# A recurrence on one core: block products of x in 384 columns on pairs of column tiles

## Chip, core and metric

One core of a Trainium2 chip. The time is that of one execution on the device, in microseconds. The engines are PE (matrix products; its weight loads are listed as PEld), DVE (vector), ACT (scalar functions and copies), POOL and SP (here it issues DMAs).

## The reference

A gated recurrence over T = 512 steps, for a batch of 8 and 512 units; its states are added to x:

```python
def step(h, x_t):
    fused = sigmoid(concatenate([x_t, h], -1) @ w_W + w_b)
    hidden_state, output_state = split(fused, 2, axis=-1)      # r and z below
    memory_state = x_t @ wx_W + wx_b + hidden_state * (h @ wh_W + wh_b)
    h_new = output_state * h + (1.0 - output_state) * tanh(memory_state)
    return h_new, h_new
return x + scan(step, cond_1024, x)        # x: (8, 512, 512) float32
```

So each step needs h @ [wh, r, z], 512 x 1536 weights, which can only start when the step before has ended, and x_t @ [wx, r, z], which depends on no state and can be done ahead.

## The kernel before

**Column tiles.** The batch is 8, so a stationary operand has few columns. PE is used as four column tiles of 32: the output's partitions 32j to 32j + 31 are tile j, which holds the units of quarter j. Each of the four tiles streams its own 128-row piece of weights as the moving operand, and they run side by side. All is float32.

**A step.** `ORDER` lists the recurrent products of step i: bank A (192 columns: half a of wh, z and r), B (128: r and wh of half b) and C (64: z of half b), each for four k (quarters of h) and four tiles j. k = 0, 1 are in `hT[0]` (hTA), k = 2, 3 in `hT[1]` (hTB). They accumulate in PSUM onto x's part, which ACT has copied there (`spread`). Then half a: DVE turns r (`tr`, L385), h (`md1`, L401) and z (`tz`); ACT takes sigmoids (md0, hd0); DVE scans give `m`, ACT takes tanh, and DVE scans give the new state (`update`, L369). Half b follows in the same way. ACT copies the new state (`hTB<-hTB`), and after that the step's extra work is issued: copies of ACT, turns and sums of DVE, sums of POOL. It thus runs while PE does the next step's A products. The order on each engine is written out by hand.

**x products.** A group `g` is four steps, 32 columns of x (4 steps x batch 8), and a block `o` is two groups, eight steps; u is the step's number in its block. The first groups are done plainly (`prefill`: 16 matmuls of 384 columns a group). From block 2 on, the 512 x 384 weights of a tile and the two groups of a block are taken as 2 x 2 blocks, and seven products with sums of weights (`tw`) and of x (`sx`, POOL, `x_sum`) replace eight. Here the weights' columns are halved within each tile: every product is 2 (k) x 4 (tiles) matmuls of 192 columns. They add into four regions, AL, BE, GA, DE, each 128 partitions by 192 columns of two PSUM banks (`xps`). `x_side` makes one long sequence of all these matmuls, and each step takes seven of it after its C products (`take(later, 7)`). Seven on four tiles are uneven, so `turn` moves the tile with which a step begins on by seven.

**Sums.** Part of the additions between regions is done in PSUM by ACT copies from region to region, part by DVE into `even` and `odd` in SBUF, from which (or from `xps`) `spread` fills the A, B and C banks and `turn_x` the x part of the memory state. The PSUM banks are A, B and C twice, for even and odd groups, and two for `xps`.

Of the kernel before, what the change touches and what calls it, by code (L numbers as in the profile page):

```python
# [40 lines left out]
def tile_cond_rnn_residual(  # L41
# [48 lines left out]
    psum = ctx.enter_context(tc.tile_pool(name="psum", bufs=1, space=PSUM))  # L90
# [43 lines left out]
    wx = const.tile([P, NQ, NQ, 384], F32, name="wx")  # L134
# [41 lines left out]
        nc.gpsimd.memset(t_[:, :, :, 1], -1.0)  # L176
    idle = const.tile([P, IDLE], F32, name="idle")

    tw = [const.tile([P, 2, NQ, HALF], F32, name=f"tw{n}") for n in range(4)]
    sx = [[const.tile([P, 2, GS * B], F32, name=f"sx{n}{q}") for q in range(2)] for n in range(4)]  # L180
    step_bias = const.tile([P, HALF], F32, name="stepbias")
    even = const.tile([P, 256], F32, name="even")
    odd = [const.tile([P, 256], F32, name=f"odd{q}") for q in range(2)]
    both = const.tile([P, HALF], F32, name="both")

    def state(hf, i, slot=2):

# [1 line left out]
        return hT[hf][i % NH][:, B * s : B * s + B, :, slot]  # L189

    ctx.enter_context(tc.manual_schedule())
    banks = [
        {n: psum.tile([P, w], F32, name=f"{n}{q}") for n, w in BANKS.items()}
        for q in range(2)
    ]
    xps = [psum.tile([P, 512], F32, name=f"xp{q}") for q in range(2)]

    def mm(out_, lhsT, rhs, start=False):
        nc.tensor.matmul(  # L199
            out_, lhsT, rhs, start=start, stop=False, skip_group_check=True  # L200
        )


    for t_ in list(banks[0].values()) + list(banks[1].values()):
        mm(t_, none, none[:, :1].broadcast_to([P, t_.shape[1]]), start=True)
    def warm():

# [4 lines left out]
    mm(xps[0], ones.rearrange("p j m -> p (j m)"), rows4, start=True)  # L212
    bias = const.tile([P, 512], F32, name="bias")
    nc.vector.tensor_copy(bias, xps[0])  # L214
# [5 lines left out]
    turn = [0]  # L220

# [11 lines left out]
    def seed(g):  # L233

        nc.scalar.copy(xps[g % 2], bias)  # L235

    def prefill(g):

        c, t0 = divmod(g * GS, TC)
        for k in range(NQ):  # L240
            for j in range(NQ):
                mm(
                    xps[g % 2][32 * j : 32 * j + 32, 64:448],
                    x_of(c, k, t0, GS),
                    wx[:, k, j, :],
                )
            yield

    def late(g):

        if g == 0:
            return xps[0][:, 256:512]
        return even if g % 2 == 0 else odd[g // 2 % 2]

    def part(g, c0, c1):

        return late(g)[:, c0 - 256 : c1 - 256] if c0 >= 256 else xps[g % 2][:, c0:c1]

    def spread(g, names):

        for n in names:
            nc.scalar.copy(banks[g % 2][n], part(g, XP[n].start, XP[n].stop))

    def turn_x(g, e):

        c0 = XP["X"].start + 32 * e
        nc.vector.transpose(md1[e // 2][g % 2][:, :, e % 2, 1], part(g, c0, c0 + 32))

    def reg(r):
        return xps[r[0]][:, r[1]]  # L270
# [8 lines left out]
    def weight_sum(n, k=slice(0, 2), j=None):  # L279
# [7 lines left out]
        at = (slice(0, P), k, slice(0, NQ) if j is None else slice(2 * j, 2 * j + 2))  # L287
        nc.vector.tensor_tensor(tw[n][at], a[at], b[at], ALU.subtract)
# [12 lines left out]
    def products(o):  # L301

        t_ = [q[o % 2] for q in sx]
        for to, lhs, rhs in (
            (AL, x_half(o, 0, 0), wx_of(0, 0)),
            (DE, t_[0], tw[0]),
            (BE, t_[1], tw[1]),
            (AL, x_half(o, 0, 1), wx_of(1, 0)),
            (GA, t_[2], tw[2]),
            (BE, t_[3], wx_of(1, 1)),  # L310
            (GA, x_half(o, 1, 1), tw[3]),
        ):
# [11 lines left out]
    def x_side():  # L324
        for o in range(2, NG // 2):
            yield from products(o)

    seed(1)
    take(prefill(0))
    warm()  # L330
    later = x_side()
    first = {g: prefill(g) for g in (1, 2, 3)}
    weight_sum(0)
    weight_sum(2)
    spread(0, "BCA")
    for e in range(NQ):
        turn_x(0, e)

    pool_done = {}
    for i in range(T):  # L340
# [8 lines left out]
        for n in (ORDER if i else FIRST).split():  # L349
            if n == "x":  # L350
                take(first[1], 1)
                continue
            bank, k = n[0], int(n[1])
            hs = hT[k // 2][i % NH][:, :, k % 2, 2]
            for j in range(NQ):
                j = (j + turn[0]) % NQ
                to = ps[bank] if i or bank != "A" else xps[0][:, XP["A"]]
                mm(to[32 * j : 32 * j + 32, :], hs, wh(bank, k, j))
        if i < 5:
            take(first[(i + 3) // 2], 2)  # L360
        else:
            take(later, 7)
            turn[0] += 7

        rows = slice(B * s, B * s + B)

# [99 lines left out]
        o, u = divmod(i, 2 * GS)  # L466
        nxt, two = o + 1 < NG // 2, o + 2 < NG // 2
        if i == 0:
            nc.scalar.copy(odd[0], xps[1][:, 256:512])
            spread(1, "A")  # L470
            turn_x(1, 0)
        ahead = 2 * o + (1 if u < 3 else 2 if u < 7 else 3)
        if ahead < NG:
            turn_x(ahead, (u + 1) % GS)
        if u == 0:
            spread(2 * o + 1, "B")
            if o and nxt:
                nc.scalar.copy(reg(GA), reg(BE))
        elif u == 1:
            spread(2 * o + 1, "C")  # L480
        elif u == 2 and o == 0:
            seed(3)
            nc.scalar.copy(even, xps[0][:, 256:512])
        elif u == 2 and nxt:
            last = odd[(o + 1) % 2][:, :HALF]
            nc.vector.tensor_tensor(last, reg(GA), both, ALU.add)
        elif u == 3 and nxt:
            if o:
                nc.vector.tensor_tensor(even[:, :HALF], reg(BE), both, ALU.add)
            spread(2 * o + 2, "A")  # L490
        elif u == 4 and nxt:
            if o == 0:
                nc.scalar.copy(odd[1], xps[1][:, 256:512])
            spread(2 * o + 2, "B")
            if two:
                nc.scalar.copy(reg(AL), bias[:, AL[1]])
                x_sum(o + 2, 0)
        elif u == 5 and nxt:
            spread(2 * o + 2, "C")
            if two:  # L500
                nc.scalar.copy(reg(DE), step_bias)
                x_sum(o + 2, 1)
        elif u == 6 and two:
            nc.scalar.copy(reg(BE), reg(AL))
            x_sum(o + 2, 2)
        elif u == 7 and nxt:
            spread(2 * o + 3, "A")
            if two:
                nc.scalar.copy(both, reg(DE))
# [3 lines left out]
        if i == 4:  # L513
            nc.gpsimd.tensor_tensor(step_bias, bias[:, BE[1]], bias[:, AL[1]], ALU.subtract)
        for n in range(IDLE - 1):
            nc.vector.memset(idle[:, n : n + 1], 0.0)
        def add(hf, engine):
# [97 lines left out]
```

## Time and profile before

| | |
|---|---|
| median of 3 runs | 1671.9 us (1671.46 to 1673.14) |
| profiled execution | 1671.53 us, its span 1669.5 us |
| granted TensorE clock | 0.999 in the mean |
| steps with block products | 496, from 38.37 to 1633.94 us |

Times in rows are microseconds from the span's start unless marked ns. A row of the timeline gives start, length, engine, line, operation, output<-inputs by the program's names, shape and count of merged instructions, and in brackets the idle time before and what ended it. A row of groups gives the count, then busy time, mean ns of one, and idle time before with what ended it. In the waits view a row gives who waited for whom, total, count and longest.

### The profile page before, as it was taken

The page shows a single profiled execution, that of the slowest core. Times are in us where ns is not written, and L with a number is a line of the kernel's source. Part 1 is how long each engine was busy: PE and PEld are TensorE (multiplying, and loading weights), DVE is VectorE, ACT ScalarE, POOL GpSimd, SP SyncE. Part 2 cuts the span into 40 slices and gives each one's busy share as a digit, 9 for nine tenths or more (in the row PEclk, how much of TensorE's full clock was granted, in tenths as well). Part 3 has the DMA queues.
Part 4 walks back from the last instruction along what each step waited for, and adds up shares of the span by engine and source line. Part 5 has one row for each costly group of instructions (what it writes and reads, how often), then busy time and mean ns, then how long its engine had stood idle before and what let it go on. Part 6 is the DMA issues. An engine that isn't in the chain of part 4 may idle for free.

```text
span 1669.5 us, 130236 instructions
## 1 busy us (share of the span) xinstructions
PE 1658.5 (99%) x56238; PEld 1639.1 (98%) x56238; DVE 1090.2 (65%) x9387; ACT 1029.7 (62%) x5822; POOL 301.7 (18%) x1281
## 2 busy tenths in 40 slices
PE   8999999999999999999999999999999999999998
PEld 5999999999999999999999999999999999999997
DVE  6666666666666666666666666666666666666666
ACT  3666666666666666666666666666666666666665
POOL 1111111111111111111111111111111111111111
PEclk9999999999999999999999999999999999999999
DMA  4000000000000000000000000000000000000000
GB/s 181 11 15 17 15 15 15 17 15 15 14 17 15 15 14 18 14 14 15 18 15 15 14 16 16 15 14 18 15 14 14 18 15 15 15 16 12 10 10 10
DMA packets 37304, 31.43 MB, mean 19 GB/s; under 512 B 4084, under 2 KB 35060, under 8 KB 36600
## 3 DMA queue, kind: packets, MB, share of 16 engines
q1 hardware_dynamic: 36576, 22.95, 4.4%
q8 instruction: 440, 7.21, 1.8%
q14 instruction: 136, 1.11, 0.2%
q10 hardware_dynamic: 152, 0.16, 0.0%
HBM read 14.70 MB, written 8.39 MB: 14 GB/s over the span
## 4 chain that ended last, share of the span: by engine, by line
PE 98%; DVE 1%; DMA 0%; issue 0%; ACT 0%
PE A L199 44%; PE B L199 23%; PE xp L199 20%; PE C L199 12%; DMA rows<-in_bias_dram 0%; DVE tr L385 0%; DVE m L369 0%; DVE tz L385 0%; DVE md1B L401 0%; DVE hTA L369 0%; DVE md1A L401 0%; DVE bias L214 0%; ACT hTB L227 0%; ACT xp L235 0%; DVE rows L131 0%
## 5 line engine op out<-in xcount | busy, mean ns | idle before, releaser
L199 PE MATMUL A<-wa,hTA 128*32 128x192 f32 x8176 | 639.0, 329 | 2.3 <-DVE hTA L369 2.3
L199 PE MATMUL B<-wb,hTA 128*32 128x128 f32 x8192 | 575.2, 273 | 0.0
L199 PE MATMUL A<-wa,hTB 128*32 128x192 f32 x8176 | 508.0, 326 | 0.4 <-DVE hTB L369 0.4
L199 PEld LDWEIGHTS B<-wb,hTA 128*32 128x32 f32 x8192 | 472.9, 122 | 1.1
L385 DVE STREAM_TRANSPOSE tr<-A 128x64 f32<-128x64 f32 x511 | 127.7, 250 | 462.5 <-PE A L199 462.5
L199 PE MATMUL B<-wb,hTB 128*32 128x128 f32 x8192 | 399.5, 273 | 0.0
L199 PEld LDWEIGHTS A<-wa,hTA 128*32 128x32 f32 x8176 | 386.8, 123 | 6.6 <-DVE hTA L369 4.0
L199 PEld LDWEIGHTS A<-wa,hTB 128*32 128x32 f32 x8176 | 373.6, 122 | 2.5 <-DVE hTB L369 0.8
L227 ACT ACTIVATE md0A<-tr 128x16 f32<-128x16 f32 x512 | 112.2, 219 | 419.9 <-DVE tr L385 419.9
L518 POOL TENSOR_TENSOR ot<-xin,hTB 128x16 f32<-128x16 f32 x503 | 125.9, 250 | 1323.4 <-DVE hTB L369 1312.9
L199 PEld LDWEIGHTS B<-wb,hTB 128*32 128x32 f32 x8192 | 322.3, 122 | 0.0
L199 PE MATMUL C<-wb,hTA 128*32 128x64 f32 x8192 | 290.2, 219 | 0.0
L199 PE MATMUL C<-wb,hTB 128*32 128x64 f32 x8192 | 289.7, 220 | 0.1
L199 PEld LDWEIGHTS C<-wb,hTA 128*32 128x32 f32 x8192 | 267.7, 122 | 0.0
L199 PE MATMUL xp<-tw,sx 128*32 128x192 f32 x2976 | 237.5, 326 | 0.0
L199 PEld LDWEIGHTS C<-wb,hTB 128*32 128x32 f32 x8192 | 229.8, 123 | 0.3 <-issue 0.3
L369 DVE TENSOR_TENSOR_SCAN hTB<-hd0B,hTB 128x24 f32<-128x24 f32 x1024 | 157.8, 196 | 100.9 <-ACT hTB L227 99.8
L369 DVE TENSOR_TENSOR_SCAN hTA<-hd0A,hTA 128x24 f32<-128x24 f32 x1024 | 191.9, 187 | 0.0
L199 PE MATMUL xp<-wx,xin 128*32 128x192 f32 (+1 forms) x2048 | 180.9, 331 | 0.0
L227 ACT ACTIVATE hd0B<-tz 128x16 f32<-128x16 f32 x512 | 115.2, 225 | 93.4 <-DVE tz L385 93.4
L227 ACT ACTIVATE hTB<-hTB 128x16 f32<-128x16 f32 x512 | 120.5, 235 | 79.8 <-DVE hTB L369 73.7
L227 ACT ACTIVATE hTB<-m 128x8 f32<-128x8 f32 x1024 | 160.6, 206 | 0.0
(92 smaller groups left out, 2491.0 us busy)
## 6 DMA issues: line engine op xcount, KB each, us to landing
out_dram<-ot SPq DMA_DIRECT2D x128, 64.0 KB, 2.0
xin<-in_x_dram SPq DMA_DIRECT2D x112, 64.0 KB, 2.5
wx<-in_wx_dram SPq DMA_DIRECT2D x4, 768.0 KB, 7.0
wa<-in_wa_dram SPq DMA_DIRECT2D x4, 384.0 KB, 8.9
wb<-in_wb_dram SPq DMA_DIRECT2D x1, 1152.0 KB
xin<-in_x_dram SPq DMA_DIRECT2D x3, 256.0 KB, 8.5
wb<-in_wb_dram SPq DMA_DIRECT2D x1, 384.0 KB, 10.9
head<-in_xh_dram ACTq DMA_DIRECT2D x1, 144.0 KB, 5.0
```

What stands on the lines that cost most here:

```text
L199: nc.tensor.matmul(out_, lhsT, rhs, start=start, stop=False, skip_group_check=True)
L227: inst = nc.scalar.activation(out_, in_, func, **kw).ins
L369: return nc.vector.tensor_tensor_scan(*[t_[:, :, c_].rearrange("p n c s -> p (n c s)") for t_ in (out_, d0, d1)], 0.0, ALU.mult, ALU.add,).ins
L385: inst = nc.vector.transpose(t_.rearrange("p c n -> p (c n)"), raw[n][hf]).ins
L518: return engine.tensor_tensor(ot[:, t, 2 * hf : 2 * hf + 2, :].rearrange("p c n -> p n c"), x_of(c, slice(2 * hf, 2 * hf + 2), t, 1).rearr ...
```

## The change

The weights' columns are no longer halved within each tile, but by tiles: the column halves of the 2 x 2 scheme are tiles 0, 1 and 2, 3 (`wx_of`). A product is then 2 (k) x 2 (tiles) matmuls of 384 columns, on the lower or the upper 64 partitions (`LO`, `HI`), and two products run side by side, one on each pair of tiles. `SLOTS` lists the seven pairs, 384 columns each. AL and GA are the lower, BE and DE the upper partitions of the two `xps` banks. One half of P5 (`E`) goes to a bank of its own, `eps`. To make room, the two C banks become one (`cs`), z of even and odd groups beside each other. `x_step` gives each step a share of columns of the sequence of slots: `SHARE`, 384 columns in steps u = 0, 1, 2 and 7 and 288 in u = 3 to 6; a piece that crosses the end of a slot is cut in two. `turn` goes.

The additions become eight ACT copies and three DVE sums of 64 x 384 per block, placed anew over the steps; `even` and `odd` hold all 512 columns, one buffer each, and every `spread` and `turn_x` reads them from SBUF (group 0 still from `xps`). `turn_x` turns 64 columns at a time, four times a block instead of eight. The sums of x on POOL move to u = 2, 3, 6 and 7. The core of the diff:

```diff
-HALF = 192
-AL, BE = (0, slice(64, 256)), (0, slice(256, 448))
-GA, DE = (1, slice(64, 256)), (1, slice(256, 448))
+W = 384
+LO, HI = slice(0, 64), slice(64, 128)
+XC = slice(64, 448)
+AL, BE, GA, DE = (0, LO), (0, HI), (1, LO), (1, HI)
+SLOTS = [
+    [("P7", 1), ("E", 1)],
+    [("P1", 0), ("P2", 0)],
+    [("P1", 1), ("P2", 1)],
+    [("P4", 0), ("P3", 0)],
+    [("P4", 1), ("P3", 1)],
+    [("P5", 0), ("P6", 0)],
+    [("P7", 0), ("P6", 1)],
+]
+SHARE = [384, 384, 384, 288, 288, 288, 288, 384]
...
+    cs = psum.tile([P, 512], F32, name="cs")
...
+         "C": cs[:, HU * q : HU * q + HU]}
...
+    eps = psum.tile([P, 512], F32, name="eps")[HI, :W]
...
+    for t_ in (even, odd):
+        nc.gpsimd.tensor_copy(t_, bias)
...
     def wx_of(kh, ch):
-        return wx[:, 2 * kh : 2 * kh + 2, :, HALF * ch : HALF * ch + HALF]
+        return wx[:, 2 * kh : 2 * kh + 2, 2 * ch : 2 * ch + 2]
...
-            for k in range(2):
-                for j in range(NQ):
-                    mm(reg(to)[32 * j : 32 * j + 32], lhs[:, k], rhs[:, k, j])
-                    yield
+    def product(o, name, k, c0, c1):
+        if not 2 <= o < NG // 2:
+            return
...
+        for j in range(2):
+            r = slice(32 * j, 32 * j + 32)
+            out_ = eps[r, c0:c1] if to is None else reg(to, slice(XC.start + c0, XC.start + c1))[r]
+            mm(out_, lhs()[:, k], rhs[:, k, j, c0:c1], start=to is None and c0 == 0)
+
+    def x_step(o, u):
+        at = sum((SHARE * 2)[4 : u if u > 3 else u + 8]) - SHARE[4] // 3
+        o += 2 if u > 3 else 1
+        end = at + SHARE[u]
+        while at < end:
+            n, c0 = divmod(at, W)
+            c1 = min(W, c0 + end - at)
+            for pair_, (name, k) in enumerate(SLOTS[n % 7]):
+                product(o + n // 7 - (n % 7 == 0 and pair_ == 0), name, k, c0, c1)
+            at += c1 - c0
...
+    weight_sum(2)
     weight_sum(0)
-    weight_sum(2)
...
-                j = (j + turn[0]) % NQ
...
-        else:
-            take(later, 7)
-            turn[0] += 7
+        if i > 3:
+            x_step(*divmod(i, 2 * GS))
...
         if u == 0:
+            spread(2 * o + 1, "AC")
+            turn_x(2 * o + 1, 0)
+            turn_x(2 * o + 1, 1)
+        elif u == 1:
+            if o and nxt:
+                nc.vector.tensor_tensor(reg(GA), reg(BE), more[HI], ALU.add)
+                nc.scalar.copy(even[LO, XC], reg(AL))
             spread(2 * o + 1, "B")
...
+        elif u == 2:
...
+                nc.vector.tensor_tensor(odd[HI, XC], reg(GA), both[LO], ALU.add)
+                nc.scalar.copy(both[HI], reg(DE))
+            if two:
+                x_sum(o + 2, 2)
+        elif u == 3:
+            if two:
+                nc.scalar.copy(reg(AL), bias[LO, XC])
+                x_sum(o + 2, 0)
+        elif u == 4:
...
+                nc.vector.tensor_tensor(even[HI, XC], reg(BE), both[HI], ALU.add)
+            if two:
+                nc.scalar.copy(reg(DE), step_bias[HI])
+        elif u == 5 and nxt:
             if o:
+                nc.scalar.copy(odd[LO, XC], reg(GA))
             spread(2 * o + 2, "A")
+            turn_x(2 * o + 2, 0)
+        elif u == 6 and nxt:
+            spread(2 * o + 2, "BC")
+            turn_x(2 * o + 2, 1)
             if two:
+                nc.scalar.copy(more[HI], eps)
+                x_sum(o + 2, 1)
+        elif u == 7 and nxt:
             if two:
+                nc.scalar.copy(reg(BE), reg(AL))
+                nc.scalar.copy(both[LO], reg(DE))
                 x_sum(o + 2, 3)
```

More of the change, by code (lines that the diff above doesn't have):

```diff
@@ L177, in tile_cond_rnn_residual @@
     idle = const.tile([P, IDLE], F32, name="idle")
-    tw = [const.tile([P, 2, NQ, HALF], F32, name=f"tw{n}") for n in range(4)]
+    tw = [const.tile([P, 2, 2, W], F32, name=f"tw{n}") for n in range(4)]
     sx = [[const.tile([P, 2, GS * B], F32, name=f"sx{n}{q}") for q in range(2)] for n in range(4)]
[L181 to L184, printed above, removed]
+    step_bias = const.tile([P, W], F32, name="stepbias")
+    both = const.tile([P, W], F32, name="both")
+    more = const.tile([P, W], F32, name="more")
+    even = const.tile([P, 512], F32, name="even")
+    odd = const.tile([P, 512], F32, name="odd")
     def state(hf, i, slot=2):
@@ L247, in prefill, with source, turn_x, reg @@
             yield
[L249 to L257, printed above, removed]
+    def source(g):
+        return xps[0] if g == 0 else (even, odd)[g % 2]
     def spread(g, names):
         for n in names:
[L262 to L270, printed above, removed]
+            nc.scalar.copy(banks[g % 2][n], source(g)[:, XP[n]])
+    def turn_x(g, hf):
+        c0 = XP["X"].start + HU * hf
+        nc.vector.transpose(
+            md1[hf][g % 2][:, :, :, 1].rearrange("p n c -> p c n"), source(g)[:, c0 : c0 + HU]
+        )
+    def reg(r, c=XC):
+        return xps[r[0]][r[1], c]
     def wx_of(kh, ch):
[L273 removed]
+        return wx[:, 2 * kh : 2 * kh + 2, 2 * ch : 2 * ch + 2]
     def x_half(o, n, kh):
         return x_of(o // 2, slice(2 * kh, 2 * kh + 2), 8 * (o % 2) + GS * n, GS)
[L279 removed]
+    def weight_sum(n, k=slice(0, 2), j=slice(0, 2)):
         a, b = [
@@ L468, in tile_cond_rnn_residual @@
         if i == 0:
[L469 to L474, printed above, removed]
-        if u == 0:
-            spread(2 * o + 1, "B")
[L477 to L487, printed above, removed]
+            nc.scalar.copy(odd[:, XC], xps[1][:, XC])
```

69 lines of the change are left out of this document (27 added, 42 removed).

## The prediction

> **What bounds the kernel now.** I read the page first (busy shares, chain, groups), then the stretch of the 496 steps with block products by windows and groups, then the timeline of single steps: one of the first, with the prefill products, one of the middle, and one of the last ten, which have no x work at all.
>
> The page, and the groups of DVE and ACT in the stretch from 38.37 to 1633.94 us (columns of a group: busy us, mean ns of one, idle before and what ended it):
>
> ```profile
> span 1669.5 us, 130236 instructions
> PE 1658.5 (99%) x56238; PEld 1639.1 (98%) x56238; DVE 1090.2 (65%) x9387; ACT 1029.7 (62%) x5822; POOL 301.7 (18%) x1281
> ...
> L199 PE MATMUL A<-wa,hTA 128*32 128x192 f32 x8176 | 639.0, 329 | 2.3 <-DVE hTA L369 2.3
> ...
> L199 PE MATMUL A<-wa,hTB 128*32 128x192 f32 x8176 | 508.0, 326 | 0.4 <-DVE hTB L369 0.4
> ```
>
> ```profile
> L385 DVE STREAM_TRANSPOSE tr<-A 128x64 f32<-128x64 f32 x497 | 124.2, 250 | 450.3 <-PE A L199 450.3
> ...
> L227 ACT ACTIVATE md0A<-tr 128x16 f32<-128x16 f32 x496 | 108.7, 219 | 401.0 <-DVE tr L385 401.0
> ```
>
> PE is never idle as a whole, and DVE and ACT wait for it in every step (450.3/497 = 0.91 us and 401.0/496 = 0.81 us). But "PE busy" is the union over four column tiles: it hides a single tile that stands still. A step has eight A matmuls on each half of h, and 8176 records are 16 in each of 511 steps: a matmul is two passes. With four column tiles, each tile runs every fourth matmul. What one pass costs on its tile is read from a step with prefill (PE's timeline, start and length in us):
>
> ```profile
> 31.40 1.47 PE L199 MATMUL xp<-wx,xin 128*32 128x384 f32 x16
> 32.69 0.51 PE L199 MATMUL A<-wa,hTA 128*32 128x192 f32 x8
> ...
> 33.55 0.83 PE L199 MATMUL A<-wa,hTB 128*32 128x192 f32 x16
> 34.20 0.40 PE L199 MATMUL B<-wb,hTA 128*32 128x128 f32 x8
> ...
> 35.31 1.15 PE L199 MATMUL xp<-wx,xin 128*32 128x384 f32 x12
> ```
>
> From start to start: 16 passes of 384 columns, four to a tile, take 32.69 - 31.40 = 1.29 us, 0.3225 us each. Four of 192 columns take 34.20 - 33.55 = 0.65, 0.1625 each. So a column costs (0.3225 - 0.1625)/192 = 0.83 ns and a pass 2 x 0.1625 - 0.3225 = 0.0025 us besides. The recurrent work of a step (A, B, C; the same before and after the change) takes 35.31 - 32.69 = 2.62 us: eight passes a tile of each width, 8 x (192 + 128 + 64) = 3072 columns at 0.83 ns and 24 x 0.0025 make the same 2.62. So where all four tiles get equal x work and enough of it, a step lasts as long as its passes, 3.91 from x to x (35.31 - 31.40), and no tile stands still. Without x work it is otherwise; the first DVE transpose dates the steps 502 and 511:
>
> ```profile
> 1637.02 0.25 DVE L385 STREAM_TRANSPOSE tr<-A 128x64 f32<-128x64 f32 x1 [0.83 <-PE A L199]
> ...
> 1664.72 0.25 DVE L385 STREAM_TRANSPOSE tr<-A 128x64 f32<-128x64 f32 x1 [0.94 <-PE A L199]
> ```
>
> (1664.72 - 1637.02)/9 = 3.078, above the 2.62 of passes: this is the recurrence (A products, transposes, sigmoids, scans, back to A). And the stretch between, 496 steps of seven 192-column matmuls:
>
> ```profile
> 38.37:1633.94 1595.57, 1595.42 (x54572) 1592.04 (x54565) 1045.54 (x9057) 995.71 (x5641) 291.46 (x1238) 1.00 0.05 15
> ```
>
> 1595.57/496 = 3.217 us a step, at full granted clock (1.00). Spread evenly, its work would be 2.62 + 14/4 x 0.1625 = 3.189. Where the other 0.028 goes is seen in one step (PE and DVE):
>
> ```profile
> 800.88 0.20 DVE L369 TENSOR_TENSOR_SCAN hTA<-hd0A,hTA 128x24 f32<-128x24 f32 x1
> ...
> 803.09 0.25 DVE L385 STREAM_TRANSPOSE tr<-A 128x64 f32<-128x64 f32 x1 [0.73 <-PE A L199]
> ```
>
> ```profile
> 801.14 0.36 PE L199 MATMUL A<-wa,hTA 128*32 128x192 f32 x1
> 801.14 0.39 PE L199 MATMUL xp<-wx,sx 128*32 128x192 f32 x2
> ```
>
> Seven matmuls on four tiles give three tiles two and the fourth one; `turn` moves the short tile round. The short tile begins A at 801.14, 0.06 after the state's scan ends (800.88 + 0.20), while x passes still start on another tile. It has waited for the chain, and its first pass takes 0.36 instead of 0.33. The groups above say that this is so in nearly every step: A<-hTA is 329 ns in the mean and A<-hTB 326, and 16 x 3 = 48 ns is about one pass prolonged by 0.04 a step. The long tiles come last, and tr waits for all four: 803.09 - 801.08 = 2.01 us from state to tr. In a step without x work, where all four tiles start as the state comes, it is 1.87 us:
>
> ```profile
> 1650.34 0.20 DVE L369 TENSOR_TENSOR_SCAN hTA<-hd0A,hTA 128x24 f32<-128x24 f32 x1
> ...
> 1652.41 0.25 DVE L385 STREAM_TRANSPOSE tr<-A 128x64 f32<-128x64 f32 x1 [0.83 <-PE A L199]
> ```
>
> So the bound is: in every step the short tile waits for the recurrence and the recurrence waits for the long tiles.
>
> **The change, part by part.** *PE.* The columns stay: 56 matmuls of 192 per eight steps over four tiles are 14 x 192 = 2688 columns a tile, and seven slots of 384 are 2688. But each piece is now four matmuls of one width, one to each tile, so no tile is short. A heavy step (share 384, u = 0, 1, 2, 7) has 2.62 + 2 x 0.3225 = 3.265 of work, a light one (288) 2.62 + 2 x (0.3225 - 96 x 0.00083) = 3.105, and u = 4 and 5, cut in two pieces, two passes more: 3.110. All lie above the recurrence's 3.078, so I take them for the steps' times, as the prefill step showed: 4 x 3.265 + 2 x 3.105 + 2 x 3.110 = 25.49 per eight steps, 3.186 each. Of the gain of 0.031, 0.0025 x (28 - 20)/8 = 0.0025 is from fewer passes, the rest from the waiting tile.
>
> *ACT.* Per eight steps five 128x192 copies become eight of 64x384. No row shows that shape. Nearest (groups by form; the first two from the stretch, the last from the whole run):
>
> ```profile
> L262 ACT COPY A<-xp 128x192 f32<-128x192 f32 x124 | 37.6, 303 | 10.3 <-DVE idle L516 10.3
> ...
> L262 ACT COPY B<-even 128x128 f32<-128x128 f32 x62 | 16.5, 266 | 0.0
> ...
> L235 ACT COPY xp<-bias 128x512 f32<-128x512 f32 x3 | 1.8, 589 | 5.3 <-DVE bias L214 5.3
> ```
>
> A new copy lies between 0.30 (as much data as 128x192) and 0.61 (twice its columns at twice its time); on the line from 192 to 512 columns it is 0.303 + 192 x (0.589 - 0.303)/320 = 0.48, which I take, since a copy's time goes by its columns in these rows. C, the narrowest, is put at B's 0.27. They sit behind the last sigmoid-side work of a step, in the time that ACT waits for tr:
>
> ```profile
> 1651.48 0.24 ACT L227 ACTIVATE hTB<-hTB 128x16 f32<-128x16 f32 x1 [0.16 <-DVE hTB L369]
> 1652.69 0.22 ACT L227 ACTIVATE md0A<-tr 128x16 f32<-128x16 f32 x1 [0.97 <-DVE tr L385]
> ```
>
> That is 0.97 us where the recurrence sets the step. What is issued at the end of step u delays the chain of u + 1, and so is set against the share of u + 1. u = 2, 3, 4 issue one copy (0.48); u = 5 one and A: 0.48 + 0.30 = 0.78; each before a light step, and under 0.97. u = 6 (B, C, one copy: 1.02) and u = 7 (two: 0.96) stand before heavy steps, where the window is 0.97 + 3.265 - 3.078 = 1.16. u = 0 (A, C: 0.57) and u = 1 (one and B: 0.75) fit as well. With 0.61 a copy, u = 5 has 0.91 and u = 6 and 7 have 1.15 and 1.22: only u = 7 is over, by 0.06, before a step whose chain has 0.187 to spare. So nothing at either end. Without this cover a step would pay the copy itself.
>
> Here the Trainium skill speaks against the change: the page TensorEngine Tiling (Array Packing), Performance Considerations, says that column tiling speeds TensorE but not the copies out of PSUM, which may then become the bottleneck. By that the sum would be that of the first rival below; in the trace before, ACT is 62% busy and waits 0.81 us a step.
>
> *DVE.* Two sums of 128x192 become three of 64x384, and eight 32-column transposes four of 64:
>
> ```profile
> L486 DVE TENSOR_TENSOR odd<-xp,both 128x192 f32<-128x192 f32 x62 | 19.6, 316 | 0.0
> ...
> L288 DVE TENSOR_TENSOR tw<-wx,tw 128x384 f32<-128x384 f32 x4 | 2.1, 517 | 0.0
> ```
>
> A sum lies between 0.32 and 0.63; I take the 384-column row, 0.52. The row at 1652.41 has 0.83 of wait left before tr, in a step that the recurrence sets, so even 0.63 fits. Cost: nothing; without that wait, each sum its length.
>
> *Waits of PE.* Seeds and sums that a product needs are written a step or more ahead: DE is seeded at the end of step u = 4, by some 1.18 + 0.48 us after the state (1651.48 + 0.24 - 1650.54), and step 5's products come 2.62 us after. The common bank for z is written by ACT before A ends, the C products come after. Both cost nothing; behind a waiting x matmul the next A would queue. POOL's x sums go one or two steps earlier, DMA stays.
>
> *Rest.* The first product (E, 192 columns) runs alone on two tiles in step 4: +0.33 us. PE also waited for instructions in the stretch,
>
> ```profile
> PEld xp L199 <- issue: 1.0, 3, 0.4
> PEld C L199 <- issue: 0.3, 1, 0.3
> ```
>
> 1.3 us that I keep. Before the first step DVE's two weight sums change places and POOL copies two tiles. At worst the first step starts one sum later, four times the 384-column row, 2.1 us; I take nothing, since PE's first products, not DVE, hold that step.
>
> *Sum.* 496 steps: 62 x 25.49 = 1580.4, with 0.33 and 1.3: 1582.0 for 1595.6, a gain of 13.6 us. The profiled execution took 1671.53 us (span 1669.5 and 2.0 around it), 0.4 under the median of 1671.9. Forecast 1671.5 - 13.6 = 1657.9 us.
>
> **The rivals.**
>
> *Light steps fall to the recurrence (slower).* If ACT's or DVE's new work makes md0A late in u = 3 to 6, a light step lasts as long as its chain, and the heavy ones don't give it back. Were it as now, 3.217: (3.265 + 3.217)/2 = 3.241, 496 x 0.024 = +12, 1683.5 us. It decides from a chain of 2 x 3.217 - 3.265 = 3.169, that is 0.09 over 3.078: an ACT load over 0.97 + 0.09 = 1.06 us in all four steps, where three have a single copy. For it: the copies work on half the partitions. Against: the 512-column copy took 0.589.
>
> *Nothing is won by even tiles.* If the 0.028 is not the short tile but something that each step has, only the passes go: 496 x 0.0025 = 1.2, 1670.3 us, no change. Against: the prefill step above has passes alone, down to 0.01.
>
> *Half of it.* The same mechanism, but short of its point: light steps halfway between their work and 3.169, at 3.14. (3.265 + 3.14)/2 = 3.202 a step, 496 x 0.015 = 7.4 less, 1664 us.
>
> *A dear pass.* If each pass carried what the restarted one shows, 0.36 - 0.33 = 0.03 us, instead of 0.0025, the eight passes fewer per tile and eight steps would give 8 x 0.03/8 x 496 = 14.9 instead of 1.2: 1644 us. Against: the two widths above leave 0.0025. The Trainium skill, page TensorEngine Tiling (Array Packing), Instruction Overhead, states some 60 cycles of overhead for each matmul; the rows here don't show it.
>
> **How the numbers follow.** Forecast 0.75, its own range 1654 to 1661 (rounding of the step's 0.01 over 496 steps is 5 us, without the waits for instructions 1.3 less); half 0.09; nothing 0.07; recurrence 0.07; dear pass 0.02. The range reaches from 1653.5 over the half case to 1667. Within 0.2% is 3.3 us, about what a measurement can tell from no change: faster 0.75 + 0.09 + 0.02 = 0.86, same 0.07, slower 0.07.
>
> **What would show it.** Right: tr to tr alternates between about 3.26 (behind heavy shares) and 3.11; in the heavy steps no A pass restarts, and A<-hTA falls to the 326 ns of A<-hTB; ACT's wait before md0A stays positive, smallest at u = 6 and 7. Wrong: light steps over 3.14, idle PE before x products, copies of 64x384 over 0.61 us, or a mean of A<-hTA still at 329 with periods of 3.217.

## The result and the profile after

The changed kernel took 1659.43 us (median of 6 runs, 1657.2 to 1660.61); the kernel before took 1672.09 in the same set (6 runs, 1671.35 to 1673.14). The ratio is 0.9922 (0.9909 to 0.9935): 12.7 us faster, where 13.6 were forecast, 1.5 us above the 1657.9 predicted and inside the range.

Where the time came from is read from the profiled execution (1659.38 us, span 1657.4), cut at first transposes (tr) of steps:

| part | before, us | after, us |
|---|---|---|
| start of the span to the first step's tr | 18.57 | 20.25 |
| tr of step 0 to tr of step 5 | 19.80 | 19.71 |
| 496 steps with block products | 1595.57 | 1581.58 |
| steps without x work | 30.78 | 30.81 |
| last tr to the end | 4.80 | 5.09 |

So the 496 steps gave 14.0 us. Their forecast was 1581.7: of the 1582.0 in the prediction, 0.33 is for the first product in step 4, which lies in the row above (that step took 4.22 us instead of 3.91). The start was counted as unchanged; its first tr came 1.7 us later, and step 5 still 1.6 later (39.95 instead of 38.37 us). The end took 0.3 more.

The page of the changed kernel, first part and its two costliest groups (busy us, mean ns of one, idle before and what ended it):

```profile
span 1657.4 us, 126070 instructions
PE 1645.1 (99%) x54253; PEld 1487.9 (90%) x54253; DVE 1152.0 (70%) x9193; ACT 1198.4 (72%) x6009; POOL 303.2 (18%) x1283
...
L217 PE MATMUL A<-wa,hTA 128*32 128x192 f32 x8176 | 547.6, 326 | 2.1 <-DVE hTA L391 2.1
L217 PE MATMUL A<-wa,hTB 128*32 128x192 f32 x8176 | 440.7, 326 | 0.0
```

PE looks just as busy as before (99%). The two things that show the change are the A<-hTA passes, 326 ns in the mean instead of 329, and the number of passes: 56238 - 54253 = 1985 less, four in each of the 496 steps (106 instead of 110). ACT is at 72% instead of 62%, DVE at 70% instead of 65%. The stretch of the 496 steps, by windows (span, then busy time of PE, PEld, DVE, ACT, POOL, granted clock, DMA share, GB/s):

```profile
39.95:1621.54 1581.59, 1581.59 (x52574) 1440.50 (x52570) 1107.03 (x8871) 1162.13 (x5825) 291.96 (x1238) 1.00 0.05 15
```

The transposes tr of steps u = 4, 5, 6, 7 and of the next u = 0, from DVE's timeline (start, length, in brackets the wait before it):

```profile
802.49 0.25 DVE L407 STREAM_TRANSPOSE tr<-A 128x64 f32<-128x64 f32 x1 [0.97 <-PE A L217]
...
805.60 0.25 DVE L407 STREAM_TRANSPOSE tr<-A 128x64 f32<-128x64 f32 x1 [0.27 <-PE A L217]
...
808.71 0.25 DVE L407 STREAM_TRANSPOSE tr<-A 128x64 f32<-128x64 f32 x1 [0.80 <-PE A L217]
...
811.82 0.25 DVE L407 STREAM_TRANSPOSE tr<-A 128x64 f32<-128x64 f32 x1 [0.83 <-PE A L217]
...
815.08 0.25 DVE L407 STREAM_TRANSPOSE tr<-A 128x64 f32<-128x64 f32 x1 [1.13 <-PE A L217]
```

Three differences of 3.11 and one of 3.26: over all 62 rounds the median steps from u = 0 on are 3.265, 3.265, 3.265, 3.105, 3.110, 3.110, 3.105 and 3.265 us, in the thousandth those of the prediction (before: 3.208 to 3.212 in every u). The 0.27 at 805.60 is the sum of 0.56 that DVE ran just before; it still had time left. PE's timeline of the step before shows why no step is longer than its passes:

```profile
800.51 0.41 PE L217 MATMUL xp<-wx,sx 128*32 128x288 f32 x2
800.72 0.53 PE L217 MATMUL A<-wa,hTA 128*32 128x192 f32 x8
801.05 0.42 PE L217 MATMUL B<-wb,hTA 128*32 128x128 f32 x8
```

There is no wait in brackets, and the eight A passes stand in one row, begun together; before, the short tile's first pass stood in a row of its own, with 0.36. Counted over all steps, one A<-hTA pass a step was prolonged in this way before, and in the median step none is now. Behind a heavy step A begins 0.25 to 0.28 us after the state, behind a light one 0.10 to 0.13; before it was 0.06 in every step. The new work of ACT and DVE, by groups in the stretch:

```profile
L246 ACT ACTIVATE md0A<-tr 128x16 f32<-128x16 f32 x496 | 108.8, 219 | 171.3 <-DVE tr L407 157.5
...
L535 ACT COPY both<-xp 64x384 f32<-64x384 f32 x62 | 29.5, 476 | 1.5
...
L499 ACT COPY even<-xp 64x384 f32<-64x384 f32 x62 | 29.3, 473 | 26.3 <-DVE idle L543 26.3
```

```profile
L407 DVE STREAM_TRANSPOSE tr<-A 128x64 f32<-128x64 f32 x497 | 124.1, 250 | 357.2 <-PE A L217 357.2
...
L498 DVE TENSOR_TENSOR xp<-xp,more 64x384 f32<-64x384 f32 x62 | 35.2, 568 | 2.0
```

ACT's wait for tr went from 401 to 171 us, DVE's for A from 450 to 357: the new copies and sums were paid out of waits. Line 499 is new: the copy into `even` waits 0.42 us each time for DVE, which the prediction did not have.

### The profile page after: what moved, and what is told of

It reads as the page before. It is cut to its first block, busy times and chain, and to the rows that moved or that the text cites. A ratio compares the mean times of both kernels' runs of the same rounds, so it can differ in the third digit from the quotient of the medians.

```text
span 1657.4 us, 126070 instructions
## 1 busy us (share of the span) xinstructions
PE 1645.1 (99%) x54253; PEld 1487.9 (90%) x54253; DVE 1152.0 (70%) x9193; ACT 1198.4 (72%) x6009; POOL 303.2 (18%) x1283
## 4 chain that ended last, share of the span: by engine, by line
PE 98%; DVE 1%; DMA 1%; issue 0%; ACT 0%; SPq 0%
PE A L217 40%; PE B L217 26%; PE xp L217 17%; PE cs L217 13%; PE eps L217 1%; DMA wx<-in_wx_dram 1%; DVE tr L407 0%; DVE m L391 0%; DVE tz L407 0%; DVE md1B L423 0%; DVE hTA L391 0%; DVE md1A L423 0%; SPq L149 0%; ACT hTB L246 0%; ACT xp L254 0%
## 5 line engine op out<-in xcount | busy, mean ns | idle before, releaser
L217 PE MATMUL B<-wb,hTA 128*32 128x128 f32 x8192 | 440.6, 273 | 0.0
L217 PEld LDWEIGHTS A<-wa,hTA 128*32 128x32 f32 x8176 | 281.3, 122 | 129.8 <-DVE hTA L391 103.7
L217 PEld LDWEIGHTS B<-wb,hTA 128*32 128x32 f32 x8192 | 337.5, 122 | 5.7
L217 PE MATMUL xp<-tw,sx 128*32 128x96 f32 x1488 | 267.5, 433 | 0.0
L217 PE MATMUL cs<-wb,hTA 128*32 128x64 f32 x8192 | 222.9, 219 | 0.0
L217 PE MATMUL cs<-wb,hTB 128*32 128x64 f32 x8192 | 222.8, 219 | 0.0
L217 PE MATMUL xp<-wx,xin 128*32 128x384 f32 (+2 forms) x1304 | 219.6, 425 | 0.0
L217 PEld LDWEIGHTS cs<-wb,hTA 128*32 128x32 f32 x8192 | 200.4, 122 | 0.0
L217 PEld LDWEIGHTS cs<-wb,hTB 128*32 128x32 f32 x8192 | 173.0, 122 | 0.0
L246 ACT ACTIVATE hTA<-m 128x8 f32<-128x8 f32 x1024 | 160.6, 206 | 2.8 <-DVE m L391 0.5
```

The costliest lines, as they stand in the source:

```text
L217: nc.tensor.matmul(out_, lhsT, rhs, start=start, stop=False, skip_group_check=True)
L246: inst = nc.scalar.activation(out_, in_, func, **kw).ins
```

## The experiments

The kernel before varies between sets of runs: 1672.09 us in the first, then 1678.58 (22 runs, 1673.39 to 1683.19), 1682.78 and 1685.84 in three sets on three chips; on which chip the first was made is not known. The changed kernel hardly does: 1659.43 in the first set, 1659.57 and 1661.04 in the last two. Ratios below are against the kernel before in the same set.

**Even tiles in the old kernel.** If the short tile is the whole cause, shares of four and eight matmuls do for the old kernel what the change does, without touching banks, copies or sums:

```
-            take(later, 7)
-            turn[0] += 7
+            take(later, (4, 8, 8, 8, 4, 8, 8, 8)[i % 8])
```

> The kernel before, with its 192-column products, but each step takes four or eight matmuls of the sequence instead of seven (4, 8, 8, 8, 4, 8, 8, 8), so that no column tile is short. Theory (a step lasts as long as the larger of its passes and the recurrence's 3.078 us): steps with eight take 2.62 + 4 x 0.1625 = 3.27, steps with four have 2.945 of passes and are lifted to 3.078; (6 x 3.27 + 2 x 3.078)/8 = 3.222 us against 3.217, 1674 to 1676 us. Rival 'even tiles alone, without a floor': 3.189 a step, 1658 us. Rival 'tiles play no part': 3.217 in all steps, 1672 us. The tr-to-tr times of single steps tell them apart: two values, 3.27 and 3.08, by the theory.

Measured: 1681.99 us (1679.76 to 1685.39), ratio 1.0023 (1.001 to 1.0036). No gain. But its steps are what even tiles give (DVE's timeline, a light and a heavy step):

```profile
811.50 0.25 DVE L384 STREAM_TRANSPOSE tr<-A 128x64 f32<-128x64 f32 x1 [0.79 <-PE A L199]
...
814.58 0.25 DVE L384 STREAM_TRANSPOSE tr<-A 128x64 f32<-128x64 f32 x1 [0.83 <-PE A L199]
...
817.85 0.25 DVE L384 STREAM_TRANSPOSE tr<-A 128x64 f32<-128x64 f32 x1 [1.02 <-PE A L199]
```

3.08 and 3.27 us; two light and six heavy steps make 3.2225 in the mean. So with equal tiles no pass is prolonged behind a heavy step. But a light step has only 2.945 us of passes, and the recurrence (3.078) sets it: behind it all four tiles wait for the state. What the heavy steps take more, the light ones don't give back. By its medians the stretch would be 1598.4 us; it was 1606.1. The other 7.7 us are single long steps, with 4.6 us of weight loads that waited for "issue", where the waits view shows nothing they waited for. That part no theory had.

**Sharper shares.** With 384 and 192 in place of 384 and 288 the light steps fall to the recurrence:

```
-SHARE = [384, 384, 384, 288, 288, 288, 288, 384]
+SHARE = [384, 384, 384, 192, 384, 192, 384, 384]
-    at = sum((SHARE * 2)[4 : u if u > 3 else u + 8]) - SHARE[4] // 3
+    at = sum((SHARE * 2)[4 : u if u > 3 else u + 8]) - 192
```

> The changed kernel with the shares 384, 384, 384, 192, 384, 192, 384, 384: the same columns in eight steps, two light steps below the recurrence. Theory: six steps at 3.265 (the cut one 3.270), two with 2.62 + 0.325 = 2.945 of passes, lifted to 3.078: 25.75 per eight steps against 25.49, 62 x 0.26 = 16 us more, 1675 to 1676 us: nearly the whole gain is gone. Rival 'only the sum of columns counts': 1659.4 us as with the change.

Measured: 1675.90 us (1675.01 to 1677.12), ratio 0.9981 (0.9971 to 0.9992). The light step of u = 3, from the timeline:

```profile
807.09 0.25 DVE L407 STREAM_TRANSPOSE tr<-A 128x64 f32<-128x64 f32 x1 [0.40 <-PE A L217]
...
810.17 0.25 DVE L407 STREAM_TRANSPOSE tr<-A 128x64 f32<-128x64 f32 x1 [0.94 <-PE A L217]
```

3.08 us, with 2.62 + 2 x 0.1625 = 2.945 of passes. As expected: time saved below 3.078 is lost, and 288 columns (3.105) stand just above that line. The other light step, u = 5, has one piece of 192 columns too, and took 3.111, not 3.078; why is not known.

**Uneven pairs.** The same columns and passes as in the changed kernel, but the upper pair of tiles runs up to 96 columns ahead of the lower one:

```
+    AHEAD = [96, 0, 0, 96, 0, 96, 0, 0]
...
+        parts = [pieces(o, 0, at, end), pieces(o, 1, at + AHEAD[u - 1], end + AHEAD[u])]
```

> The changed kernel with its shares, but the upper pair of tiles runs 96 columns ahead after steps u = 3, 5 and 0 and gives them back in the next step; columns and order within a pair of tiles are the same. Theory: after u = 3 and 5 the lower tiles finish 0.16 us before the upper ones, find the next state not ready in the step after, and wait: from 3.105 + 3.110 = 6.215 to about 6.345 for each two steps, twice in eight; after u = 0 (heavy steps) the slack of 0.2 takes it. 62 x 0.26 = 16 us more, 1675 us. Rival 'evenness in a step doesn't matter, the sums of columns over a block do': 1659 to 1660 us.

Measured: 1671.55 us (1670.82 to 1672.81), ratio 0.9955 (0.9942 to 0.9968), 12 us more than the changed kernel in the first set. The timeline, a step whose pairs have 288 and 384 columns and the next, with 288 and 192:

```profile
805.90 0.25 DVE L419 STREAM_TRANSPOSE tr<-A 128x64 f32<-128x64 f32 x1 [0.39 <-PE A L217]
...
809.14 0.25 DVE L419 STREAM_TRANSPOSE tr<-A 128x64 f32<-128x64 f32 x1 [1.09 <-PE A L217]
...
812.22 0.25 DVE L419 STREAM_TRANSPOSE tr<-A 128x64 f32<-128x64 f32 x1 [0.24 <-PE A L217]
```

3.24 + 3.08 = 6.32 us where the changed kernel takes 6.215: the longer pair sets one step, the recurrence the other. Eight median steps sum to 25.714 instead of 25.490, and 62 x 0.224 = 14 us in this profile. This is the mechanism of the prediction by itself: the work is the same (106 passes a step in both), only its spread over the tiles differs. (Expected was 3.265 where 3.24 came, hence 1675 for 1671.55.)

**More passes.** Each piece cut into two of half the width: the same columns, 116 passes a step instead of 106.

```
+            mid = (c0 + c1) // 2
             for pair_, (name, k) in enumerate(SLOTS[n % 7]):
-                product(..., name, k, c0, c1)
+                product(..., name, k, c0, mid)
+            for pair_, (name, k) in enumerate(SLOTS[n % 7]):
+                product(..., name, k, mid, c1)
```

> The changed kernel with each piece of x products cut in two halves of its width (192, 144, 96 and 48 columns): 40 passes a tile in eight steps instead of 20, the columns the same. Theory (a pass costs 0.0025 us besides its columns): 20 x 0.0025 = 0.05 us per eight steps, 62 x 0.05 = 3 us more, 1662.5 us. Rival 'a pass is dear' (0.03 us as the restarted one): 62 x 0.6 = 37 us more, 1697 us. If wide columns rather than even tiles made the gain, it would be gone: 1671 us.

Measured: 1747.56 us (1746.87 to 1750.78), ratio 1.0412 (1.0386 to 1.0437). Every expectation missed, the dear pass by 50 us. The medians say that a pass costs its tile what it should: 3.270 and 3.110 in five of the eight steps. The steps of u = 4, 5 and 6 are 3.260, 3.607 and 3.563. The waits from 45 to 1630 us (who waited, for what; total us, times, longest):

```profile
PEld cs L217 <- issue: 20.3, 47, 0.9
...
PEld xp L217 <- issue: 15.8, 41, 0.9
```

With 12.4 for B, 10.4 for A and 2.8 for eps that is 61.7 us of the weight loads' "issue", of 87 us that the stretch lasts longer. The passes are not even over the steps: u = 4 and 5 have 128, the others 112, and the two longest steps are u = 5 and the one behind it. It made a new theory: PE as a whole runs out of instructions when steps have too many passes, and that, beside the tiles, is what the change relieves.

**The changed kernel and the one before, again.** Controls for the runs beside them, and for the issue waits in other sets.

> The changed kernel once more, as the measure for the three beside it on the same chip: 1659 us, tr to tr 3.265 behind heavy and 3.105 to 3.110 behind light shares. What the kernel before takes beyond its own 1672 on this chip would be waits of PE for instructions, of which the changed kernel (106 passes a step against 110) should have few.

> The kernel before once more, for its profile on the chip on which the others run. Beside the experiments it took 1678.6 and 1682.8 us, 7 and 11 us more than the 1672 of the first chip, where the changed kernel took 1659.6 as on the first. Theory (PE waits for instructions, since the kernel before has 110 passes a step and the changed one 106): most steps last 3.21 us as in the first profile, and PE's weight loads show waits put down to issue of several us in the stretch of products, against 1.3 in the first profile; the steps over 3.3 us carry the difference. Rival 'the recurrence or the passes are slower on these chips': the middle step is longer than 3.21.

The changed kernel took 1659.57 us (1659.16 to 1662.3), its weight loads waiting 1.4 us for issue. The kernel before took 1686.32 in one run of the slowest set, stretch 1610.18 instead of 1595.57. Its median step there is 3.220, but 55 of 480 steps last over 3.3 us, against 7 in the first set. Its two largest issue waits:

```profile
PEld C L199 <- issue: 4.6, 13, 0.6
PEld xp L199 <- issue: 4.3, 15, 0.5
```

9.6 us in all, where the first set had 1.3; and the stretch lies 13 us over its median steps, 3.5 in the first set. The median step is 3.22 against 3.21. So the sets differ by some 10 us in single long steps and by 5 in the median step. The passes are no slower there: on that chip the changed kernel's median steps are the same as in the first set.

**Passes alone.** Only the 384-column pieces of the changed kernel cut into 192 + 192: as many passes as before (110), tiles even, everything else of the change kept.

```
             c1 = min(W, c0 + end - at)
+            if c1 - c0 == W:
+                c1 = W // 2
```

> The changed kernel with only its 384-column pieces cut in two of 192: 28 passes a tile in eight steps, as many as the kernel before (110 a step for PE) and as wide, but even over the tiles. Theory of even tiles: 8 x 0.0025 = 0.02 us per eight steps, 1.2 us more than the changed kernel, besides waits for instructions. Theory of instruction supply (from the 116 passes a step that took 88 us more): at 110 the waits are those of the kernel before on the same chip, some 5 to 10 us. So 1661 us if the chip supplies them as the first did, 1666 to 1671 if not; in either case the middle steps are at 3.27 and 3.11. Rival 'wide columns make the gain': middle steps back at 3.21, 1672 us or more.

> The changed kernel again, as the measure for the runs beside it: 1659 to 1660 us, its middle steps at 3.265, 3.105 and 3.110; the first tr at 18.5 us or, where the clock was lost in the wait for the weights, 20.2.

Measured in one set: 1677.19 us (1674.89 to 1680.7) for the cut pieces, ratio 0.9952 (0.9937 to 0.9968); 1661.04 (1659.46 to 1662.21) for the changed kernel, ratio 0.9854 (0.9841 to 0.9868). Both expectations for the cut pieces missed low. The median steps are 3.270, 3.105 and 3.110, so the passes' price and the even tiles hold; by them the stretch is 1581.6 us, and it was 1598.7. The largest waits for issue of the cut pieces:

```profile
PEld cs L217 <- issue: 3.8, 13, 0.5
PEld xp L217 <- issue: 2.9, 11, 0.5
PEld A L217 <- issue: 1.9, 8, 0.3
```

With two smaller rows that is 9.5 us, against 1.5 in the changed kernel, and 17 against about 3 in long steps. In this set the change gained 24.8 us: 8.6 with the number of passes as before (1685.84 to 1677.19; the median steps alone give 15.4, and longer waits and the start take some of it back), and 16.2 by fewer and wider passes, of which the arithmetic of the prediction had 1.2. Fewer and wider come together here; no run parts them.

**More copies on ACT.** Does ACT's new work come near the point where it decides? One more copy of 64x384, of no use to the result, in both u = 3 and u = 4, or in u = 5 alone (there as shown; in the other `u in (3, 4)`):

```
+        if i > 8 and u == 5:
+            nc.scalar.copy(extra[LO], bias[LO, XC])
```

> The changed kernel with one more ACT copy of 64x384 (of no use to the result) at the end of steps u = 3 and u = 4, 124 copies of 0.47 us in all. Theory (copies lie in ACT's wait for tr): after the change that wait is 0.63 us in step 4 and 0.50 in step 5, so the copies fit, by 0.15 and 0.02: no change, 0 to 2 us more than the changed kernel. Rival 'the copies out of PSUM are the bottleneck' (each copy is paid): 124 x 0.47 = 58 us more.

> The changed kernel with one more ACT copy of 64x384 (of no use to the result) at the end of step u = 5 alone, 62 copies. There ACT has 0.13 us left before md0A of step 6, so md0A comes 0.35 late, and the state with it; the next A has about 0.07 of slack. Theory: step 6 to 7 grows from 3.105 by about 0.28 to 0.32 with the restart, 62 times: 17 to 20 us more than the changed kernel. Rival 'ACT is off the path altogether': no change. Rival 'every copy is paid': 29 us more.

At u = 3 and 4: 1662.53 us (1660.0 to 1664.09), ratio 0.9871 (0.9847 to 0.9896) against 0.9862 (0.9841 to 0.9883) for the changed kernel in the same set, so no difference that is resolved. No median step changed; the wait before md0A went from 0.63 to 0.18 in step 4, and from 0.50 to nothing in step 5. At u = 5: 1670.96 us (1670.5 to 1671.65), ratio 0.9927 (0.9907 to 0.9947), 11.4 more. ACT's timeline:

```profile
912.86 0.22 ACT L247 ACTIVATE md0A<-tr 128x16 f32<-128x16 f32 x1 [0.50 <-DVE tr L408]
...
915.52 0.32 ACT L276 COPY A<-even 128x192 f32<-128x192 f32 x1
915.78 0.51 ACT L539 COPY extra<-bias 64x384 f32<-64x384 f32 x1
916.19 0.21 ACT L247 ACTIVATE md0A<-tr 128x16 f32<-128x16 f32 x1
...
919.27 0.22 ACT L247 ACTIVATE md0A<-tr 128x16 f32<-128x16 f32 x1 [0.17 <-DVE tr L408]
```

md0A at 916.19 has no wait: ACT is late, and 3.33 us lie between it and the last instead of 3.11. The step behind it is 3.293 instead of 3.105 in the median, 62 x 0.188 = 11.7 us, the whole difference. Expected were 17 to 20. The copy used up the 0.13 us of wait that this step had and made md0A 0.22 late, 0.35 in all and not its own 0.48: it begins before the copy ahead of it has ended, and md0A before it has. So ACT's work is hidden, but at u = 5 with less than one copy to spare.

**The start.** The changed kernel's first tr came at 20.25 us instead of 18.57. The window from 15 to 19 us before and after (columns as above):

```profile
15.00:19.00 4.00, 3.94 (x83) 3.03 (x86) 0.43 (x3) 0.15 (x1) 0.00 (x0) 1.00 1.00 402
```

```profile
15.00:19.00 4.00, 3.95 (x40) 2.25 (x44) 0.00 (x0) 0.00 (x0) 0.00 (x0) 0.57 0.98 398
```

The granted clock is 0.57 after and 1.00 before, and 40 passes are done instead of 83. PE's timeline after:

```profile
11.94 1.13 PE L217 MATMUL xp<-zeros 128*128 128x512 f32 x2
15.05 0.86 PE L217 MATMUL xp<-wa,hTA 128*32 128x192 f32 x8 [1.99 <-issue]
```

PE rests for 1.99 us (before: 0.25) ahead of the first A product. The next two experiments were made in the belief that it waits there for the recurrent weights. The traces show another cause: the weights of that product land at 12.0 us, and PE waits on for a semaphore that DVE counts up at 14.96, at the end of its transposes of x's part of group 0, which lies in the same bank. The product's first weight load begins 0.07 us after the last of them, in thirteen of the fourteen profiles (all but the one with five matmuls of zeros). DVE's timeline after, and that of the kernel before in its later profile:

```profile
11.23 3.43 DVE L302 TENSOR_TENSOR tw<-wx 128x1536 f32<-128x1536 f32 x2 [2.01 <-DMA wx<-in_wx_dram]
...
14.74 0.21 DVE L280 STREAM_TRANSPOSE md1B<-xp 128x64 f32<-128x64 f32 x1
```

```profile
9.15 1.75 DVE L288 TENSOR_TENSOR tw<-wx 128x1536 f32<-128x1536 f32 x1
11.61 1.76 DVE L288 TENSOR_TENSOR tw<-wx 128x1536 f32<-128x1536 f32 x1 [0.71 <-DMA wx<-in_wx_dram]
...
13.52 0.27 DVE L267 STREAM_TRANSPOSE md1B<-xp 128x32 f32<-128x32 f32 x2
```

The change swapped the two weight sums. The one that needs the last weights of x now comes first, so both run after these have landed, where one was done before. The first A product starts at 14.9 to 15.3 us, against 13.9 in the two profiles of the old start that kept the clock. (In the profile of the table above the old kernel also started it at 15.05, since its prefill ran at a clock of 0.50 from 9.23 to 12.64 us.) Two kernels fill the rest with more products of zeros; none puts the sums back in their old order:

```
     prefill(0)
-    warm()
+    for _ in range(5):        # in the second kernel: 3
+        warm()
```

> The changed kernel with four more of the matmuls of zeros that follow the first prefill, in the 2 us in which PE waits for the recurrent weights before step 0. In the profile after, the granted clock was 0.53 to 0.62 from 15 to 19 us and the first tr came at 20.25 us, where the kernel before had a clock of 1.00 and 18.57. Theory (PE stood still and lost its clock): the clock stays at 1.00 through step 0 and the time falls by 1.7 us. Rival 'the later start has another cause': no change. If the matmuls outlast the load, it is slower by what they overrun.

> The changed kernel with two more matmuls of zeros before step 0 instead of four: one took 0.9 us (two passes of 0.45), so three end at about 14.8 us, before the recurrent weights are there at 15.0. Theory (PE at rest loses its clock in some runs: of the profiles of the changed kernel one lost it and one did not): the first tr comes at 18.5 us at full clock every time, and the time is 0 to 1.7 us under that of the changed kernel in the same rounds.

Five: 1661.61 us (1660.91 to 1662.78), ratio 0.9872 (0.9852 to 0.9892), 2.0 more than the changed kernel beside it. The clock held, but the zeros overran:

```profile
12.10 4.56 PE L217 MATMUL xp<-zeros 128*128 128x512 f32 x10
16.59 0.55 PE L217 MATMUL xp<-wa,hTA 128*32 128x192 f32 x8
```

Each is two passes of 0.45 us; I had counted one. Three: 1659.85 us (1658.7 to 1660.44), ratio 0.9847 (0.9834 to 0.9861) against 0.9854 (0.9841 to 0.9868). The profile has the clock at 1.00 from 15 to 19 us and the first tr at 18.52, but so have four of the nine profiles without these products. The medians differ by 1.2 us and the intervals overlap, so a gain is not shown.

## Why the prediction was right, and where it was not

*The short tile.* Right, by its own numbers: steps of 3.265, 3.105 and 3.110, A<-hTA at 326 ns, no prolonged pass behind a heavy step, 1581.58 us for 1581.7. The uneven pairs show the mechanism alone (12 us for the same passes), the sharper shares that the light step must stay above 3.078.

*ACT.* The copy was taken at 0.48 and took 0.45 to 0.48; it costs nothing, as said. The place of the smallest wait was wrong. The prediction said u = 6 and 7; the medians of the wait before md0A are 0.10 and 0.13 us in steps 2 and 6, behind the items of u = 1 and u = 5, and 0.20 and 0.19 in steps 7 and 0. The step that failed is the list of copies by u: it added ACT's own lengths and left out that the copy into `even` waits 0.42 us for DVE's sum. It had 0.19 to spare behind u = 5 (0.97 - 0.78), where 0.13 was measured.

The Trainium skill, TensorEngine Tiling (Array Packing), PSUM Bottleneck, says that copies out of PSUM may bound a kernel with column tiles. Here they don't (ACT 72% busy, 0.35 us of wait a step). One copy more at u = 5, which reads SBUF but takes as long, and ACT sets that step.

*DVE.* Sums of 0.55 to 0.57 us instead of 0.52, still before A ends. POOL's x sums do not all go "one or two steps earlier": one goes four earlier, one a step later.

*The start.* "I take nothing, since PE's first products, not DVE, hold that step" failed in its reason: DVE's sums hold it, by the very swap that the prediction named. That the late sum itself costs nothing lasting is luck. In the two old profiles with a full clock PE waits 0.7 us for wb soon after, and step 5's tr comes at 38.42 and 38.46 us; in the four profiles of the changed start that kept the clock it comes at 38.37 to 38.52. In the five that lost the clock in the rest before the first A product it comes at 39.78 to 40.23. The prediction asked when the first products may begin, not at what clock.

*The issue waits.* "1.3 us that I keep" is the step that is wrong in kind, though the first set did not show it. They are no constant of the kernel: in the slowest set they went from 9.6 to 1.5 us with the passes, and there they and the other long steps are worth about as much as the even tiles. The forecast of 13.6 holds for the set whose profile it was read from; in the two others the change gains 23.2 us (1682.78 to 1659.57) and 24.8.

*The rivals.* Light steps at the recurrence and nothing won by even tiles fell with the steps' medians. The dear pass fell in its form: a pass costs its tile 0.0025 us in every kernel here, which agrees with the fixed 2.5 ns for each warm matmul in the Trainium skill, TensorE: Matmul & The Clock Gate, section "Wait — 56ns, not 53.3ns?". What is dear is more passes than PE as a whole gets instructions for (last section).

## What to carry to other kernels

When PE shows 99% busy with column tiles, look at single tiles: a tile that is short of work restarts late, and the others set the step, so give each tile the same columns in each step and keep each step just above the recurrence. Count the passes of a step beside their time, since wide ones cost no more per column, and a few too many cost more than ten times their arithmetic here. When sums at the start change places, ask what waits for the second one, what PE does meanwhile, and at what clock it will begin.

## What the hardware showed that was not expected

*A limit on passes.* Issue waits of the weight loads from 45 to 1630 us, by passes a step: 106: 0.2 to 1.5 us in the changed kernel, up to 3.3 in its variants; 110: 1.3 us in the first set, 4.6, 9.6 and 9.5 in others; 116: 61.7 us. (The uneven pairs, with 106, show 12.6: one short wait in every eight steps, of another kind.) The mean rate, passes a step over the mean step, comes to 34.5 passes a us with 116 (1668.8/496 = 3.365 us), 34.0 with 110 in the old kernel with even tiles (1606.1/496 = 3.238), 34.2 in the kernel before, and 33.2 to 33.3 with 106, which its columns set. So something near 34 passes a us, a matmul with its weight load every 29 ns, is as fast as instructions came here over many steps.

Over short stretches PE is faster. In the kernel before, 32 passes of 64 columns begin in 0.45 us (34.86 to the next start, 35.31):

```profile
34.86 0.41 PE L199 MATMUL C<-wb,hTA 128*32 128x64 f32 x16
35.08 0.41 PE L199 MATMUL C<-wb,hTB 128*32 128x64 f32 x16
```

The Trainium skill, TensorE: Matmul & The Clock Gate, section "Wait — 56ns, not 53.3ns?", states that matmuls never start less than about 25 ns apart. Across column tiles it is not so here: these start 14 ns apart in the mean, so that floor is not the limit.

What holds PE up is its next block of instructions. The page of a profile counts the packets of a DMA queue of instructions (packets, MB, share), for the kernel before, the changed one, and the halved pieces:

```profile
q8 instruction: 440, 7.21, 1.8%
```

```profile
q8 instruction: 424, 6.95, 1.7%
```

```profile
q8 instruction: 463, 7.59, 1.9%
```

A packet is 16 KB, and in all three there is one for every 256 of PE's matmuls and weight loads (2 x 56238 = 440 x 255.6 before). By the trace's records of these packets, all 231 issue waits of the weight loads in the five profiles with 110 or 116 passes end 1.16 to 1.64 us after a packet has landed, where only 13% of all weight loads begin. With the halved pieces, 143 of the 144 distances between one such wait and the next are a multiple of 128 weight loads, to within two. The packets came every 3.71 us there in the mean, where the columns alone would have used one up in 3.52. What sets the packets' pace, and whether it is the chip or the time that makes sets differ, stays open.

*A clock that is lost by where a rest falls.* Of nine profiles with the changed start, five have the first tr at 20.08 to 20.53 us and four at 18.47 to 18.76, all with the same rest of 1.99 us. The Trainium skill, TensorE: Matmul & The Clock Gate, Part 1, describes a free-running window of about 3.4 us of activity, into which one rest can fall differently from run to run. The traces agree. In each of the five the granted clock falls to 0.50 for 3.41 or 3.42 us, and this begins 10.24 us, three times 3.41, after it first came up to 1.00. Cut into windows of 3.41 us from that moment, the whole rest lies in one window in all five, and is split between two in all four that kept the clock. Windows of one profile of each kind (columns as above; the first pair is of one that lost it):

```profile
11.71:15.12 3.41, 1.42 (x10) 0.39 (x10) 3.24 (x4) 0.59 (x3) 0.00 (x0) 1.00 1.05 429
15.12:18.53 3.41, 3.41 (x32) 1.85 (x36) 0.00 (x0) 0.00 (x0) 0.00 (x0) 0.50 1.00 406
```

```profile
10.10:13.52 3.42, 2.37 (x18) 0.46 (x10) 2.39 (x2) 0.59 (x3) 0.00 (x0) 1.00 1.02 410
13.52:16.93 3.41, 1.98 (x33) 1.37 (x37) 1.33 (x3) 0.00 (x0) 0.00 (x0) 1.00 1.04 434
```

With PE busy for 1.42 us of a window the clock was lost, with 1.98 it was kept. Where the first window begins differs from run to run (4.88 to 7.78 us in the nine), and what sets it is not known.
